# The opening norms of a two-layer kernel: fills moved to VectorE, a fixed order, and half of the norms moved into the loop

## The chip, the cores and the metric

The kernel runs on one core of one Trainium2 chip. Its engines are TensorE (PE in the profile; its weight loads are PEld), VectorE (DVE), ScalarE (ACT), GpSimd (POOL) and SyncE (SP, which only issues transfers). The engines run their own instruction streams in order and meet at semaphores. The metric is the device time of one execution in microseconds, lower is better; the time quoted is the median of several executions. A profile is one execution; its span runs from the first to the last instruction, and its time is a little longer than the span.

## The reference

The input `x` has 2 sequences of 1024 tokens with 128 features. Two pre-norm layers follow. Everything is float32. What this document turns on is the very first step and the layer that uses it:

```python
def _layernorm(x, axis=-1, eps=1e-05):
    m = jnp.mean(x, axis=axis, keepdims=True)
    v = jnp.var(x, axis=axis, keepdims=True)
    return (x - m) / jnp.sqrt(v + eps)
...
    x = x + _L0_attn_ref(_layernorm(x, axis=-1), ...)   # 16 heads of 64, causal
    x = x + _L0_ffn_ref(_layernorm(x, axis=-1), ...)    # a dense map and one of four low-rank maps for each token
    x = x + _L1_attn_ref(_layernorm(x, axis=-1), ...)   # 16 heads of 8, scores from squared distances
    x = x + _L1_ffn_ref(_layernorm(x, axis=-1), ...)    # a shared expert and 2 of 8 experts for each token
```

## The kernel before

Tokens are kept in tiles of 128 (16 tiles, 8 for each sequence) and in groups of four tiles, 512 tokens (four groups: 0 and 1 are the first sequence, 2 and 3 the second). The kernel has three parts.

**The opening** loads `x` and the weights, normalises `x`, turns weights around with TensorE, and projects the first unit. A unit is a pair of heads of one sequence, so each sequence has 8 units. The instructions of the opening are ordered by the framework's scheduler. `layernorm_T(b)` does the two groups of one sequence: for each of four token tiles `bn_stats` and `bn_aggr` (L134, L135), then the reciprocal square root (`rsqrt`: `bound` on DVE, L99; `guess` on ACT, a logarithm and an exponential, L102 and L103; `refine` on DVE, four small operations, L106 to L109), then for each tile the normalised tile `xn` (L141) and its transposition by TensorE (L145), and one copy of the four out of PSUM to `xnT` (L146). The opening calls it for the first sequence, projects the first unit from that (`project`, whose matmuls are all at the helper line L69, and whose results q, k and v leave PSUM at L432, L440 and L448), and calls it for the second sequence. `turn_nat` turns the 24 tiles of the q, k and v weights (L331) and copies them to `wqkvT` (L336, L338). `small_weights` turns and combines the other weights, with small results handed between PE, DVE, ACT and POOL (L153 to L409); its last result is `m2` (`m` in the profile, L409). `sides_of_rows` makes four small columns `side_of` for layer 1 from a tile `row`, which POOL zeroes, sets in parts and multiplies by the identity (L343 to L350), and DVE sums (L351). `fill(own[0], G)` zeroes 22 of every 32 columns of a big tile for layer 1 on POOL (L182, L183), and does not depend on anything.

PSUM is dealt out anew between the opening and the loop: the opening has four banks `tr` for transposed tiles and four `acc`; the loop has `sc`, `flip`, `z` and one bank `acc`. So the first matmul of the loop (`scp<-k,q`) waits until the last bank of the opening has been read out, which is the copy to `m2`.

**Layer 0's loop** is ordered by hand (`manual_schedule`), one step for each item; an item is a head pair's row block of 128 queries, `it["i"]` is the number of that block (0 to 7), and there are 128 items, those with `i` of 4 to 7 and of 0 to 3 taking turns. Each step runs the scores, the softmax (DVE L478, ACT L482, POOL L494), the transposition of the weights two steps later (`flip`, PE L512, copies L517), the sum with v (`zp`, L541), and in its last part one of three things in the bank `acc`: the end of a unit (`finish`), or the next piece of the next unit's projection (`later`), but none of these in a step whose `i` is 5. The second layer norm, the feed-forward part and the third norm of finished token tiles are dealt out over later steps as `events`, with the same `rsqrt_parts`.

**Layer 1** follows, attention and then the experts.

The queues matter for what follows. SP issues the loads of `x`, of the k weights, `proj`, the five plain weights, `wd` (four pieces), `wu` (eight pieces), and last `sim`, `bp` and `temp` (L309, L311, L313). POOL issues small loads too, as part of its own stream.

Of the kernel before, what the change touches and what calls it, by code (L numbers as in the profile page):

```python
# [14 lines left out]
P = 128  # L15
# [5 lines left out]
def two_layers(ctx: ExitStack, tc: tile.TileContext, a: dict, out: bass.AP):  # L21
# [40 lines left out]
    def tr():  # L62
        return bank("tr").rearrange("p o (j q) -> p (o j) q", q=P)
# [60 lines left out]
    def rsqrt(*of):  # L124
        for part in rsqrt_parts(*of)[:3]:
            part()


    def layernorm_T(b):
        for g in range(b * NG // B, (b + 1) * NG // B):  # L130
            mv = small.tile([P, 4, 2], FP, tag="mv", name="mv")
            for j in range(4):
                st = small.tile([P, V.BN_STATS_DIM], FP, tag="st", name="st")
                V.bn_stats(st, x[:, 4 * g + j, :])  # L134
                V.bn_aggr(mv[:, j, :], st)  # L135
            rstd = small.tile([P, 4], FP, tag="rstd", name="rstd")
            rsqrt(rstd, mv[:, :, 1], EPS, ALU.add)
            t = tr()
            for j in range(4):
                xn = work.tile([P, D], FP, tag="xn", name="xn")  # L140
                V.tensor_scalar(  # L141
                    xn, x[:, 4 * g + j, :], mv[:, j, 0:1], rstd[:, j : j + 1],
                    ALU.subtract, ALU.mult,
                )
                T.transpose(t[:, j, :], xn, ident)  # L145
            V.tensor_copy(xnT[:, bass.ts(g, 512)], t.rearrange("p j q -> p (j q)"))  # L146
# [92 lines left out]
    with ExitStack() as l0:  # L239
# [28 lines left out]
        def load_nat(eng, i, cs):  # L268
            w = a[f"L0_attn_W{'qkv'[i]}"].rearrange("h d e -> (h d) e").rearrange("(c p) e -> p c e", p=P)
            eng.dma_start(nat[i][:, cs, :], w[:, cs, :])  # L270

        for i in range(3):
            load_nat(nc.scalar, i, slice(0, 1))
        bnat = stage.tile([2 * NC, P], FP, name="bnat")
# [8 lines left out]
        load_nat(nc.scalar, 2, slice(1, NC))  # L283
        vnat = stage.tile([H, 2, DH], FP, name="vnat")
# [23 lines left out]
        simI = stage.tile([NP, 4 + NP], FP, name="simI")  # L308
        nc.sync.dma_start(simI[:, :4], a["L0_ffn_sim"])  # L309
        bp = stage.tile([NP, 1], FP, name="bp")  # L310
        nc.sync.dma_start(bp, a["L0_ffn_bp"].unsqueeze(1))  # L311
        temp = stage.tile([P, 1], FP, name="temp")
        nc.sync.dma_start(temp, a["L0_ffn_temp"].partition_broadcast(P))  # L313
# [25 lines left out]

        def sides_of_rows():  # L340

            row = stage.tile([P, 4, 4, 32], FP, name="row")
            G.memset(row, 0.0)  # L343
            for k, part, value in (
                (0, slice(0, DK), 1.0), (0, slice(DK + 1, DK + 2), 1.0), (1, slice(DK, DK + 1), 1.0),
                (2, slice(0, DK), 2.0), (2, slice(DK, DK + 1), 1.0), (3, slice(DK + 1, DK + 2), 1.0),
            ):
                G.memset(row[:, k, :, part], value)
            row = row.rearrange("p k h j -> p k (h j)")
            G.tensor_tensor(row, row, bcast(ident, 1, [P, 4, P]), ALU.mult)  # L350
            V.tensor_reduce(side_of, row, AX.X, ALU.add)  # L351
# [409 lines left out]
        turn_nat(*[(i, [0]) for i in range(3)])  # L761
# [3 lines left out]
        layernorm_T(0)  # L765
        for piece in project(units[0]):
            piece()
        layernorm_T(1)
# [6 lines left out]
        sides_of_rows()  # L775
# [11 lines left out]
        fill(own[0], G)  # L787
# [4 lines left out]
        while n < len(items) + LAG or longs or shorts or ends or later:  # L792
# [42 lines left out]
            elif later and not (it and it["i"] == 5):  # L835
                later.pop(0)()
            if old and old["i"] % 2:
                (longs if old["i"] >= 4 else shorts).extend(attend(old["group"]))
# [724 lines left out]
```

## Time and profile before

| | |
|---|---|
| time, median of 3 runs | 1074.09 us (1072.64 to 1076.69) |
| the profiled execution | time 1072.64 us, span 1070.9 us, mean granted TensorE clock 0.987 |
| busy in the span: PE / DVE / ACT / POOL | 1002.2 / 588.8 / 688.7 / 340.8 us |
| first matmul of the projection | starts at 17.67 us |
| first matmul of layer 0's loop | starts at 40.13 us |
| PE busy from 0 to 40 us, in stretches of 10 us | 1.68, 4.38, 9.73, 7.15 us |

The profile's page gives each engine's busy time and the span in 40 slices; further views give the chain of work that ended last (for each step the one before it that released it), a timeline in order of time, and groups of instructions by line and shape. In a group's row the numbers after the bar are the busy time in us and the mean of one instruction in ns. In a timeline row they are the start, the length in us, the engine, line and operation, output and inputs with partitions x elements, and how many instructions are merged into the row. Times of busy PE are modelled at their ends.

### The profile page before, as it was taken

Reading aid. Unit: us, or ns where it says so; the run is one execution under the profiler, and the core shown is the slowest. Engines: PE = TensorE matmul, PEld = TensorE weight load, DVE = VectorE, ACT = ScalarE, POOL = GpSimd, SP = SyncE. Lnnn points to the kernel's source line nnn. Section 1 sums busy time; section 2 is a strip of 40 time slices with the busy share of each in tenths; the row PEclk is TensorE's granted clock in tenths of the full one; section 3 lists DMA queues with packets and bytes.
Section 4 is the critical chain, followed back from the end, with each engine's and each line's share of the span. In section 5 each row is a group of like instructions: output and inputs, shape, how many; then the busy total and the mean of one; then the engine's idle time right before and its main releaser. Section 6 shows DMA issues by size and latency. Waiting matters only on the chain.

```text
span 1070.9 us, 26194 instructions
## 1 busy us (share of the span) xinstructions
PE 1002.2 (94%) x10662; PEld 603.2 (56%) x10662; DVE 588.8 (55%) x1758; ACT 688.7 (64%) x1312; POOL 340.8 (32%) x480
## 2 busy tenths in 40 slices
PE   4899999999999999999898989999999999899996
PEld 2466767667676676666666323323333332689885
DVE  7676677786877868686684333301434320455424
ACT  2376766666666666665465776888776778475651
POOL 4143343434444344444353020000000222005676
PEclk9799999999999999999999999999998999999999
DMA  5000000000000000000000500000000100011222
GB/s 131 1 2 2 2 2 2 2 2 2 2 3 2 2 2 2 2 2 1 2 2 15 164 1 2 1 1 1 21 2 6 28 18 19 1 40 46 70 72 75
DMA packets 27590, 20.13 MB, mean 19 GB/s; under 512 B 3715, under 2 KB 25070, under 8 KB 27470
## 3 DMA queue, kind: packets, MB, share of 16 engines
q1 hardware_dynamic: 22366, 12.17, 4.1%
q0 software_dynamic: 2816, 5.17, 1.7%
q8 instruction: 84, 1.38, 0.5%
q10 hardware_dynamic: 2288, 1.12, 0.4%
q14 instruction: 36, 0.29, 0.1%
HBM read 13.34 MB, written 5.11 MB: 17 GB/s over the span
## 4 chain that ended last, share of the span: by engine, by line
PE 75%; DVE 10%; ACT 7%; issue 3%; POOL 3%; DMA 2%; DVEq 0%; SPq 0%; POOLq 0%; ACTq 0%
PE accp L69 24%; PE bigp L69 14%; PE scp L69 11%; PE zp L69 10%; PE flipp L512 8%; PE trp L69 3%; ACT pT L517 2%; PE upp L69 2%; POOL back L1460 2%; ACT p L482 1%; DVE pT L517 1%; DMA xs<-rows,from 1%; PE trp L1217 1%; DVE p L478 1%; PE trp L208 1%
## 5 line engine op out<-in xcount | busy, mean ns | idle before, releaser
L1189 ACT ACTIVATE e<-bigp 128x1024 f32<-128x1024 f32 x256 | 247.7, 1021 | 79.6 <-PE bigp L69 66.5
L494 POOL TENSOR_SCALAR p<-p,rz 128x384 f32<-128x384 f32 (+7 forms) x256 | 188.2, 749 | 289.7 <-DVE rz L491 261.5
L482 ACT ACTIVATE p<-p,nmax 128x384 f32<-128x384 f32 (+7 forms) x256 | 196.3, 769 | 25.3 <-DVE nmax L478 24.5
L478 DVE CUSTOM_DVE_ANT_0 p<-scp,mask 128x384 f32<-128x384 f32 (+7 forms) x256 | 183.4, 753 | 28.0 <-PE scp L69 16.5
L517 ACT COPY pT<-flipp 128x128 f32<-128x128 f32 (+7 forms) x128 | 81.5, 636 | 146.9 <-PE flipp L512 140.0
L69 PE MATMUL scp<-k,q 64*128 64x512 f32 (+3 forms) x768 | 163.6, 505 | 0.5 <-DVE m L409 0.5
L69 PE MATMUL bigp<-rT,lT 32*128 32x512 f32 x1024 | 158.0, 643 | 0.0
L69 PEld LDWEIGHTS zp<-pT,v 128*64 128x64 f32 x2560 | 136.2, 137 | 26.9 <-issue 8.3
L69 PE MATMUL zp<-pT,v 128*64 128x128 f32 (+1 forms) x2560 | 146.5, 265 | 1.8 <-DVE zT L541 1.1
L512 PEld LDWEIGHTS flipp<-ident,p 64*128 64x128 f32 x2304 | 92.1, 139 | 97.9 <-issue 47.2
L69 PE MATMUL accp<-e,own 128*32 128x512 f32 x1024 | 140.5, 611 | 0.0
L517 DVE COPY pT<-flipp 128x128 f32<-128x128 f32 (+7 forms) x128 | 96.0, 750 | 58.7 <-PE flipp L512 58.5
L512 PE MATMUL flipp<-ident,p 64*128 64x64 f32 x2304 | 111.1, 229 | 17.8 <-DVE rz L491 14.5
L1053 POOL DMA_INDIRECT xs<-rows,from x46 | 45.6, 991 | 239.2 <-DVE top L1073 156.9
L69 PEld LDWEIGHTS bigp<-rT,lT 32*128 32x128 f32 x1024 | 50.6, 183 | 108.2 <-issue 71.5
L69 PEld LDWEIGHTS scp<-k,q 64*128 64x128 f32 x768 | 69.9, 190 | 38.0 <-issue 30.8
L69 PE MATMUL accp<-xnT,wqkvT 128*64 128x512 f32 x256 | 71.7, 627 | 1.7 <-ACT o L619 0.8
L1316 ACT ACTIVATE hs<-upp,w 128x128 f32<-128x128 f32 x176 | 50.3, 369 | 33.3 <-PE upp L69 16.3
L69 PEld LDWEIGHTS accp<-e,own 128*32 128x32 f32 x1024 | 20.9, 108 | 65.4 <-issue 64.6
L432 ACT ACTIVATE q<-accp,bqk 128x512 f32<-128x512 f32 x32 | 37.2, 1163 | 29.7 <-PE accp L69 29.1
L1206 DVE COPY cs<-accp 128x512 f32<-128x512 f32 x16 | 11.0, 690 | 73.0 <-PE accp L69 73.0
L541 DVE TENSOR_TENSOR zT<-zp,bz 128x256 f32<-128x256 f32 x64 | 38.7, 605 | 20.9 <-PE zp L69 20.6
(330 smaller groups left out, 1148.2 us busy)
## 6 DMA issues: line engine op xcount, KB each, us to landing
given<-y SPq DMA_DIRECT2D x10, 256.0 KB, 2.3
wx<-in_L_ffn_We_dram SPq DMA_DIRECT2D x1, 2048.0 KB
wx<-in_L_ffn_We_dram SPq DMA_DIRECT2D x8, 256.0 KB, 4.0
x<-in_L_attn_x_dram SPq DMA_DIRECT2D x4, 256.0 KB, 4.0
rows<-xn SPq DMA_DIRECT2D x4, 256.0 KB, 2.3
out_dram<-x SPq DMA_DIRECT2D x3, 256.0 KB, 2.3
xs<-rows,from POOLq DMA_INDIRECT x46, 2.5
proj<-in_L_attn_proj_dram SPq DMA_DIRECT2D x1, 512.0 KB
```

The costliest lines, as they stand in the source:

```text
L69: T.matmul(o, lhsT=lhsT, rhs=rhs, start=start, stop=stop)
L432: S.activation(q[:, 4 * j : 4 * j + 4].rearrange("p i r u -> p i u r"), t.rearrange("p (i u r) -> p i u r", r=2, u=DH), AF.Identity, bias= ...
L478: V.tensor_tensor_reduce(out=p[:, :n], in0=it["sc"][hh], in1=mask[:, SEQ - n :], scale=1.0, scalar=-NEG, op0=ALU.add, op1=ALU.min, accum_o ...
L482: S.activation(p[:, :n], p[:, :n], AF.Exp, bias=nmax, scale=-1.0, accum_out=it["sum"][:, hh : hh + 1],)
L494: G.tensor_scalar(p[:, :n], p[:, :n], r[:, hh : hh + 1], SC, ALU.mult, ALU.mult)
L512: T.transpose(it["t", hh][:, r, j, :], it["p"][hh][rs, bass.ts(j, P)], ident[rs, rs])
L517: copy(it["group"]["pT", hh][:, : i + 1, i % 2].rearrange("p j r u -> p r j u"), it["t", hh])
L541: V.tensor_tensor(zT[:, :, :, 16 * g : 16 * g + 16].rearrange("p m h q -> p h q m"), z.rearrange("p (h q m) -> p h q m", h=2, m=M2), bz[:, ...
L1053: G.indirect_dma_start(out=r["xs"][q][:, j, :], out_offset=None, in_=rows[b][:, :], in_offset=bass.IndirectOffsetOnAxis(ap=r["from"][:, i ...
L1189: S.activation(e[:, 2 * pr : 2 * pr + 2, :], sc[pr], AF.Exp, scale=1.0 / math.sqrt(DK))
L1316: S.activation(h[:, f, :], t[:, f, :], AF.Silu, bias=w[:, I + NF * D + f : I + NF * D + f + 1])
L1460: G.indirect_dma_start(out=returned[b, j][:, k, :], out_offset=None, in_=given[b][:, :], in_offset=bass.IndirectOffsetOnAxis(ap=routed[b][ ...
```

## The change

It has four parts.

1. `fill(own[0], V)`: the big tile's fill is issued at the start of the opening, on VectorE. The tile `row` is zeroed and set in parts on VectorE as well; its product with the identity stays on GpSimd, now near the head of its stream. The sum `side_of` stays on VectorE.
2. The loads of `sim`, `bp` and `temp` go from the end of SP's queue to GpSimd's, ahead of its other small loads.
3. In the opening only groups 0 and 1 are normalised. `norm_T(g)` returns three parts (statistics and guess; refine, normalise and transpose; copy). They are issued with VectorE and ScalarE in a fixed order: both groups' statistics first, then group 0, with the first three weight tiles between, then group 1.
4. Groups 2 and 3 are normalised in layer 0's loop by `norm_later`: one piece in each step after the eighth whose `i` is below 4 (a tile's statistics, or the guess, or one tile normalised into a free part of `xn2T`), and the four transpositions with ScalarE's copy in the bank `acc`, in a step in which neither `finish` nor `later` uses it.

The core of the diff, in the changed kernel's order (the old `layernorm_T`, `sides_of_rows` and the three SP loads are taken out):

```diff
+    def norm_T(g):
+        mv = small.tile([P, 4, 2], FP, tag="mv", name="mv")
+        rstd = small.tile([P, 4], FP, tag="rstd", name="rstd")
+        bound, guess, refine = rsqrt_parts(rstd, mv[:, :, 1], EPS, ALU.add)[:3]
+        t = []
+
+        def stats():
             for j in range(4):
                 st = small.tile([P, V.BN_STATS_DIM], FP, tag="st", name="st")
                 V.bn_stats(st, x[:, 4 * g + j, :])
                 V.bn_aggr(mv[:, j, :], st)
+            bound()
+            guess()
+
+        def normal():
+            refine()
+            t.append(tr())
             for j in range(4):
                 xn = work.tile([P, D], FP, tag="xn", name="xn")
                 V.tensor_scalar(
                     xn, x[:, 4 * g + j, :], mv[:, j, 0:1], rstd[:, j : j + 1],
                     ALU.subtract, ALU.mult,
                 )
+                T.transpose(t[0][:, j, :], xn, ident)
+
+        def keep():
+            V.tensor_copy(xnT[:, bass.ts(g, 512)], t[0].rearrange("p j q -> p (j q)"))
...
+    def norm_later(g, room):
...
+        def guess():
+            stats(3)
+            w["rstd"] = small.tile([P, 4], FP, tag="rstd", name="rstd")
+            w["parts"] = rsqrt_parts(w["rstd"], w["mv"][:, :, 1], EPS, ALU.add)
+            w["parts"][0]()
+            w["parts"][1]()
+
+        def normal(j):
+            if not j:
+                w["parts"][2]()
+            V.tensor_scalar(
+                room[:, bass.ts(j, P)], x[:, 4 * g + j, :], w["mv"][:, j, 0:1], w["rstd"][:, j : j + 1],
+                ALU.subtract, ALU.mult,
+            )
+
+        def turn():
+            t = spare[0]()
+            for j in range(4):
+                T.transpose(t[:, j, :], room[:, bass.ts(j, P)], ident)
+            spare[1](xnT[:, bass.ts(g, 512)], t.rearrange("p j q -> p (j q)"))
+
+        each = lambda f, js: [lambda j=j: f(j) for j in js]
+        return each(stats, range(3)) + [guess] + each(normal, range(4)) + [turn]
...
         for i in range(3):
             load_nat(nc.scalar, i, slice(0, 1))
+        fill(own[0], V)
+
+        row = stage.tile([P, 4, 4, 32], FP, name="row")
+        V.memset(row, 0.0)
...
+            V.memset(row[:, k, :, part], value)
+        row = row.rearrange("p k h j -> p k (h j)")
+        G.tensor_tensor(row, row, bcast(ident, 1, [P, 4, P]), ALU.mult)
...
+        nc.gpsimd.dma_start(simI[:, :4], a["L0_ffn_sim"])
...
+        nc.gpsimd.dma_start(bp, a["L0_ffn_bp"].unsqueeze(1))
...
+        nc.gpsimd.dma_start(temp, a["L0_ffn_temp"].partition_broadcast(P))
...
-        turn_nat(*[(i, [0]) for i in range(3)])
+
+        with tc.manual_schedule(engines={mybir.EngineType.DVE, mybir.EngineType.Activation}):
+            one, two = norm_T(0), norm_T(1)
+            one[0]()
+            two[0]()
+            one[1]()
+            turn_nat(*[(i, [0]) for i in range(3)])
+            one[2]()
+            two[1]()
+            two[2]()
         transposed(bqk, bnat)

         V.tensor_scalar(bqk[:, :NC], bqk[:, :NC], -SC, None, ALU.mult)
-        layernorm_T(0)
         for piece in project(units[0]):
             piece()
-        layernorm_T(1)
...
-        sides_of_rows()
+        V.tensor_reduce(side_of, row, AX.X, ALU.add)
...
-        fill(own[0], G)
+        norms = []
+        for g in range(NG // B, NG):
+            norms += [(False, f) for f in norm_later(g, xn2T[:, bass.ts(g, 512)])]
+            norms[-1] = (True, norms[-1][1])
...
             elif later and not (it and it["i"] == 5):
                 later.pop(0)()
+            elif norms and norms[0][0]:
+                norms.pop(0)[1]()
+            if norms and not norms[0][0] and it and it["i"] < 4 and n > NB:
+                norms.pop(0)[1]()
```

The order of the instructions on each engine, as built, adds three things that the diff alone doesn't tell. On DVE the operations on `simI` and `temp` (the tiles of the loads that change queue) stand inside the norms: `simsq`, which reads `sim`, stands behind the first of group 1's refine operations, and the one on `temp` ahead of group 1's last `xn`. On PE the first head of the first projection stands ahead of group 1's first three transpositions, and the second head behind them; then two q weight tiles, group 1's last transposition, five more q tiles and three k tiles, then the other six of the projection's matmuls. In the loop, TensorE gets four transpositions of `xn2T` into `accp` at two places, and nothing else is moved there.

More of the change, by code (lines that the diff above doesn't have):

```diff
@@ L126, in rsqrt @@
             part()
-    def layernorm_T(b):
-        for g in range(b * NG // B, (b + 1) * NG // B):
-            mv = small.tile([P, 4, 2], FP, tag="mv", name="mv")
+    def norm_T(g):
[4 more added lines that the diff above has]
+        def stats():
             for j in range(4):
@@ L135, in layernorm_T @@
                 V.bn_aggr(mv[:, j, :], st)
-            rstd = small.tile([P, 4], FP, tag="rstd", name="rstd")
-            rsqrt(rstd, mv[:, :, 1], EPS, ALU.add)
-            t = tr()
+            bound()
[3 more added lines that the diff above has]
+            t.append(tr())
             for j in range(4):
@@ L144, in layernorm_T, with stats @@
                 )
-                T.transpose(t[:, j, :], xn, ident)
-            V.tensor_copy(xnT[:, bass.ts(g, 512)], t.rearrange("p j q -> p (j q)"))
+                T.transpose(t[0][:, j, :], xn, ident)
+        def keep():
+            V.tensor_copy(xnT[:, bass.ts(g, 512)], t[0].rearrange("p j q -> p (j q)"))
+        return stats, normal, keep
+    def norm_later(g, room):
+        w = {}
+        def stats(j):
+            if not j:
+                w["mv"] = small.tile([P, 4, 2], FP, tag="mv", name="mv")
+            st = small.tile([P, V.BN_STATS_DIM], FP, tag="st", name="st")
+            V.bn_stats(st, x[:, 4 * g + j, :])
+            V.bn_aggr(w["mv"][:, j, :], st)
+        def guess():
[5 more added lines that the diff above has]
+        def normal(j):
+            if not j:
+                w["parts"][2]()
[10 more added lines that the diff above has]
+        return each(stats, range(3)) + [guess] + each(normal, range(4)) + [turn]
     def transposed(dst, src):
@@ L273, in two_layers @@
             load_nat(nc.scalar, i, slice(0, 1))
+        fill(own[0], V)
+        row = stage.tile([P, 4, 4, 32], FP, name="row")
+        V.memset(row, 0.0)
+        for k, part, value in (
+            (0, slice(0, DK), 1.0), (0, slice(DK + 1, DK + 2), 1.0), (1, slice(DK, DK + 1), 1.0),
+            (2, slice(0, DK), 2.0), (2, slice(DK, DK + 1), 1.0), (3, slice(DK + 1, DK + 2), 1.0),
+        ):
+            V.memset(row[:, k, :, part], value)
+        row = row.rearrange("p k h j -> p k (h j)")
+        G.tensor_tensor(row, row, bcast(ident, 1, [P, 4, P]), ALU.mult)
         bnat = stage.tile([2 * NC, P], FP, name="bnat")
@@ L283, in two_layers @@
         load_nat(nc.scalar, 2, slice(1, NC))
+        simI = stage.tile([NP, 4 + NP], FP, name="simI")
+        nc.gpsimd.dma_start(simI[:, :4], a["L0_ffn_sim"])
+        bp = stage.tile([NP, 1], FP, name="bp")
+        nc.gpsimd.dma_start(bp, a["L0_ffn_bp"].unsqueeze(1))
+        temp = stage.tile([P, 1], FP, name="temp")
+        nc.gpsimd.dma_start(temp, a["L0_ffn_temp"].partition_broadcast(P))
         vnat = stage.tile([H, 2, DH], FP, name="vnat")
@@ L307, in two_layers @@
                 )
[L308 to L313, printed above, removed]
         nc.gpsimd.dma_start(wr1, a["L1_ffn_Wr1"])
@@ L338, in turn_nat @@
                 V.tensor_copy(wqkvT[:, :, cs[0] * P : (cs[0] + 1) * P], t[:, :at, :])
[L340 to L351, printed above, removed]
         def small_weights():
```

## The prediction

> **What bounds the kernel now.** I read the page first, then the chain of waits of the opening and of the loop, then the timelines of DVE and POOL for the first 45 us. The page says that TensorE is the bound of the whole:
>
> ```profile
> PE 1002.2 (94%) x10662; PEld 603.2 (56%) x10662; DVE 588.8 (55%) x1758; ACT 688.7 (64%) x1312; POOL 340.8 (32%) x480
> ```
>
> That mean hides the opening. There the chain is DVE's until 17.6 us (start, length, what):
>
> ```profile
> 8.94 0.17 DVE rsq L99
> 9.10 0.21 DVE rsq L106 x3
> 9.31 0.22 DVE rsq L107 x3
> 9.53 3.92 DVE rsq L108 x3
> 13.45 0.03 DVE rstd L109
> 13.47 1.31 DVE rstd L109 x2
> 17.67 1.97 PE accp L69 x2
> 22.65 4.47 PE accp L69 x44
> 30.18 2.60 DVE wqkvT L336 x5
> 39.70 0.30 DVE m L409
> ```
>
> Operations on 4 columns take 3.92 and 1.31 us here. In POOL's timeline the same stretches are its fills and its product:
>
> ```profile
> 9.98 0.54 POOL L343 MEMSET row<- 128x512 f32 x1
> 10.44 2.46 POOL L182 MEMSET own<- 128x2816 f32 x1
> 12.83 0.35 POOL L348 MEMSET row<- 128x32 f32 x6
> 13.49 1.27 POOL L350 TENSOR_TENSOR row<-row,ident 128x512 f32<-128x512 f32 x1
> ```
>
> L108 ends at 13.45 as the fills end, L109 at 14.78 as the product ends (14.76): DVE is held by POOL for about 5 us, with everything behind it. In the loop the chain of 75 to 250 us has DVE for under 3%:
>
> ```profile
> by line: PE scp L69 26.3%; PE zp L69 26.0%; PE accp L69 19.8%; PE flipp L512 18.6%; ACT pT L517 4.0%; issue 1.5%; DVE pT L517 1.0%; DVE rz L491 0.6%; ACT p L482 0.6%; DVE rsq L107 0.4%; DVE rsq L106 0.3%; DVE p L478 0.2%; DVE st L571 0.1%;
> ```
>
> **The fills on DVE.** DVE's own fills give the price:
>
> ```profile
> L369 DVE MEMSET ones<- 32x128 f32 x1 | 0.2, 165 | 0.9 <-PEq L1549 0.9
> L385 DVE MEMSET brow<- 128x51 f32 x1 | 0.1, 101 | 0.0
> ```
>
> 77 elements more cost 64 ns, so 0.83 ns each and 0.06 us fixed (1.04 ns if the fixed part is 0.04 us). 2816 elements are 2.4 to 3.0 us, I take 2.9; `row` 0.55, the 128-element piece 0.1, six small pieces 0.4. DVE starts at 0.89, so ends near 4.9, where before it began the statistics at 4.00 when `x` had landed. Cost 0.9 us.
>
> **The opening in the fixed order.** A dependent `bn_stats` and `bn_aggr` take 0.42 us a tile (the loop's pair at 633.01 is followed by the next at 633.43), against 0.26 us interleaved in the opening now. Eight tiles with two bounds: 4.9 + 3.6 = 8.5. ACT's guess of group 0 (two of 0.2 us) hides under group 1's statistics. `refine` is four dependent steps of 0.2 (18.30, 18.48, 18.68 show the spacing): 9.35. Three `xn` at 0.26 (rows 0.34 long, overlapping): 10.1; `side_of` 0.6 (the row is 0.67, POOL's product done at about 6.3): 10.7; the fourth `xn`: 11.0; the copy of the first weight tiles 0.5 (row 0.54): 11.5; `xnT` 0.7 (row 0.69): 12.2. The first head's matmul starts at 12.25 instead of 17.67, 5.4 us earlier.
>
> Then PE's order decides. The first head took 1.97 us alone at 17.67, so 14.2; three transpositions and the bias 1.1 (L145 x3 took 0.99 at 15.10): 15.3; the second head 1.97 if TensorE is as slow as at 20.19, 1.1 if it is as fast as after 22.6 (two heads together took 1.08 at 47.31). Two q tiles and group 1's last transposition 0.3 to 0.6, the copy 0.7, three k tiles behind it (their bank is freed by that copy) 0.4: the six other matmuls start between 18.15 and 19.2, where now it is 22.58. Gain 3.9, the middle; ends 3.4 and 4.4.
>
> The rest of the projection is unchanged and ends at 27.05 now. From there to the end of the `wqkvT` copies DVE has 5.65 us (to 32.7): two `xnT`, three `xn`, six copies. Afterwards the q tiles are copied earlier and the second sequence isn't there; four copies stay (0.6, 0.5, 0.6, 0.5) and 0.2 for the first tile: 2.4. Gain 3.25 more, together 7.15. From 32.7 to 40.13 the chain of small weights is the same hand-to-hand work, 7.4 us, and the loop starts near 33.0.
>
> **The loads that change queue.** POOL issues them behind the product and `mask`, at about 7.0, 7.6 and 8.1. POOL's loads issued at 7.18 to 8.20 landed after 5.9 to 6.0 us, in the crowded first 15 us; `sim` and `temp` on SP took 1.6 and 2.6 late in the opening. So they land at 13.0 and 14.1. Behind `simsq` on DVE wait the other three refine steps of group 1, and PE for their tiles; but PE has the first head until 14.2, and the tiles come at 13.6 to 14.4. Cost nothing; without that cover each us of delay costs one. If they land as late as POOL's slowest (6.5 us and issued a us later), 1.5 us are lost.
>
> **The loop.** Eight transpositions go from the opening to a loop that TensorE bounds. Seven tiles took 0.93 us at 27.43: 0.13 each, 1.05 us. Statistics 8 x 0.42 and `xn` 8 x 0.34 are 6.1 us of DVE over some 170 us in which DVE is busy 75%; I cost them at nothing, hidden under PE's matmuls; statistics are never held (259 to 293 ns, 32 of L571). The small operations can be: L106 and L107 together are 0.7% of 175 us on the chain, 1.2 us for the three or four norms in it, 0.35 a set. Two sets: 0.7. ACT's two copies (0.57, the row of v) fall in steps with an empty `acc`: nothing, at worst 0.6 each. Sum 1.75; bounds 0.8 (half the transpositions hidden, half the holds) and 6.
>
> **Sum.** -7.15 + 1.75 = -5.4: a span of 1065.5 and a time of 1067.2 for an execution like the profiled one (1072.64, the fastest shown, 1.45 under the median). Against the median 1074.09 I predict 1068.6, 0.5% less. A measurement of this kernel can tell 0.5% (5.4 us) from no change; the forecast lies on that edge.
>
> [...] The clock row comes first:
>
> ```profile
> 32.00:33.00 1.00, 0.49 (x3) 0.31 (x2) 1.00 (x5) 0.00 (x0) 0.00 (x0) 0.81 0.05 16
> 33.00:34.00 1.00, 1.00 (x4) 0.54 (x3) 0.79 (x6) 0.00 (x0) 0.00 (x0) 0.50 0.00 0
> 46.00:47.00 1.00, 1.00 (x10) 0.52 (x8) 0.36 (x2) 0.90 (x1) 0.07 (x1) 0.86 0.00 0
> ```
>
> (the seventh number is the granted clock) shows half speed from 32.6 to about 46.3, so 6.1 us of the loop run slow. [...]
>
> For the loads the row is POOL's 5.9 us against SP's 1.6. [...]
>
> **The rivals.**
> *Late loads* (0.12): `sim` lands past 14.2 and DVE stands at `simsq`. For: nothing else in the fixed order can pass it, and POOL's last load (6.5 us) was slower than all but three of SP's (`raw_w` 7.8, `raw_wp` 7.4, `raw_wv` 6.6). Against: 13.0 by the nearest rows. Priced at 2 to 3 us: about 1071.
>
> *The loop pays for all* (0.25): the transpositions, ACT's copies and some held `xn` reach PE, 4 us instead of 1.75: 1071. For: `xn` copies SBUF to SBUF like the operations held at 9.53. Against: DVE waits 24.0 us for `flip` in that window, so there is slack.
>
> *Held norms in the loop turn the change over* (0.09): L99, L106 and L107 have single instances of 1020, 942 and 1025 ns, 0.85 above the least. Eighteen operations (eight `xn`, two bounds, eight of refine) held that long and all passed on to PE are 15.3 us: -7.15 + 1.05 + 15.3 = +9.2, 1083. Slower than before as soon as more than 6.1 us of the holds pass through. Against: the medians of L106 and L107 on `rstd` are 155 and 161 ns, so most are not held.
>
> *The fill still holds someone* (0.05): if DVE's fill keeps POOL out as POOL's kept DVE out, POOL's product starts later, near 7.5, and blocks the first refine: 1 to 2 us, 1070. Either way the 5 us hold is gone.
>
> **How the numbers follow.** The forecast as it stands has 0.49. Its own spread, 1 us from the second head, 1 from the phase, 1 from the loop, puts it half on either side of the 0.5% edge, towards the faster side where ACT and DVE are wholly hidden (1066) and the opening takes its upper end (1065). Faster by over 0.5%: 0.47; within: 0.44 (the rest of the forecast and the first, second and fourth rivals); slower by over 0.5%: 0.09, the third. Range 1064 to 1075: the best ends of opening and loop, up to a loop that takes back the whole gain.
>
> **What would show it.** In the changed profile: no operation of L106 to L109 over 0.3 us before 15 us; DVE's fills from 0.9 to 4.9; the first projection matmul at 12.2, the six others at 18 to 19, the loop at 33. POOL's product at 5 to 6.3. `simsq` without a wait for its load. In the loop, PE's chain longer by 1 to 2 us between 75 and 250, `xn` at 0.34 or held. It would be wrong if the loop starts later than 35, or if the loop, from its start to the end, is longer by over 3 us.

## The result, and the profile after

The kernel after takes 1067.91 us (median of 4 runs, 1067.13 to 1069.35), the kernel before in the same comparison 1075.39 (1072.64 to 1076.75): a ratio of 0.994, 95% interval 0.9922 to 0.9958. The profiled executions have spans of 1066.4 and 1070.9 us, so the two traces that are compared below are 4.5 us apart, where the medians are 7.5 us apart: the trace before is the fastest of its four executions.

TensorE's busy time in the summary of the kernel after is what it was (1002.2 us before):

```profile
PE 1001.5 (94%) x10662; PEld 604.1 (57%) x10662; DVE 588.9 (55%) x1765; ACT 689.2 (65%) x1314; POOL 338.5 (32%) x474
```

The chain of waits of its opening (start, length, what):

```profile
1.47 2.40 DVE own L228
...
8.61 0.18 DVE rsq L108
8.81 0.17 DVE rstd L109
...
12.29 1.97 PE accp L69 x2
...
15.30 1.90 PE accp L69 x2
...
18.60 4.47 PE accp L69 x44
23.37 2.23 DVE wqkvT L393 x4
...
32.18 0.30 DVE m L453
32.62 0.80 PE scp L69 x4
```

The operations of L108 and L109 that took 3.92 and 1.31 us now take 0.18 and 0.17. The first projection matmul starts at 12.29 (17.67 before), the other six heads' at 18.53 by the timeline (22.58), the loop's first scores at 32.62 (40.13). That is 7.5 us by the loop's start. GpSimd's product, beside which L109 stood before, now runs while VectorE has only statistics to do, whose `bn_stats` take 0.26 us each beside it (timeline of GpSimd, the bracket is the idle time ahead of it and who ended it):

```profile
4.87 1.26 POOL L330 TENSOR_TENSOR row<-row,ident 128x512 f32<-128x512 f32 x1 [1.83 <-DVE row L328]
```

The loop gives some of it back. The chain of the loop from 75 to 250 us:

```profile
by line: PE zp L69 25.6%; PE scp L69 24.4%; PE accp L69 19.4%; PE flipp L556 17.3%; ACT pT L561 4.0%; issue 2.0%; DVE pT L561 2.0%; PE accp L188 0.7%; ACT p L526 0.6%; DVE p L522 0.6%; DVE rz L535 0.6%; DVE rsq L107 0.5%; DVE rsq L99 0.5%; 
```

New in it is `accp L188`, the eight transpositions: 0.7% of 175 us, 1.2 us. VectorE's operations of the norms are on this chain for about 4 us, summed over their lines, where they were for 2 before; L99 and the normalising (L180) are most of the difference.

How far the kernel after is ahead at the same piece of work (the last addition to `x` of a unit, and layer 1's start and end) shows where the rest went:

| point | before, us | after, us | ahead by |
|---|---|---|---|
| loop's first scores | 40.13 | 32.62 | 7.51 |
| unit 5 finished | 262.73 | 256.61 | 6.12 |
| unit 11 finished | 465.94 | 459.67 | 6.26 |
| unit 15 finished | 586.03 | 580.31 | 5.72 |
| end of the span | 1070.93 | 1066.44 | 4.49 |

No instruction that the change moved into the loop runs behind unit 11. What takes 1.8 us there are two stretches of 3.4 us at half the granted clock that the profile before does not have: at the same instructions the lead falls from 6.24 to 5.72 us across the first and from 5.73 to 4.54 across the second, and from there to the end it stays between 4.5 and 5.1. The windows of the kernel after show them (stretch, its length, the busy time of PE, PEld, DVE, ACT and POOL, the granted clock, the DMA share, GB/s):

```profile
467.80:471.20 3.40, 1.40 (x18) 0.74 (x13) 3.19 (x11) 0.55 (x2) 1.83 (x3) 1.00 0.00 0
471.20:474.60 3.40, 3.10 (x34) 2.68 (x36) 1.70 (x6) 1.91 (x5) 1.35 (x2) 0.51 0.00 0
631.60:635.10 3.50, 1.60 (x18) 0.34 (x10) 0.65 (x4) 3.47 (x6) 0.87 (x2) 1.00 0.00 0
635.10:638.50 3.40, 3.32 (x20) 0.93 (x20) 0.42 (x1) 0.05 (x1) 2.05 (x10) 0.50 0.00 0
```

A window in which TensorE was busy for 1.40 of 3.40 us is followed by one at half clock. In the kernel before the same dip falls between two windows, none of them so empty, and nothing follows:

```profile
472.90:476.30 3.40, 2.54 (x38) 1.70 (x34) 3.16 (x13) 1.69 (x5) 2.89 (x4) 1.00 0.00 0
476.30:479.70 3.40, 1.80 (x34) 1.55 (x36) 2.83 (x7) 1.21 (x3) 1.43 (x3) 1.00 0.00 0
```

### The profile page after: what moved, and what is told of

It reads as the page before. It is cut to its first block, busy times and chain, and to the rows that moved or that the text cites. A ratio compares the mean times of both kernels' runs of the same rounds, so it can differ in the third digit from the quotient of the medians.

```text
span 1066.4 us, 26197 instructions
## 1 busy us (share of the span) xinstructions
PE 1001.5 (94%) x10662; PEld 604.1 (57%) x10662; DVE 588.9 (55%) x1765; ACT 689.2 (65%) x1314; POOL 338.5 (32%) x474
## 4 chain that ended last, share of the span: by engine, by line
PE 75%; DVE 10%; ACT 6%; issue 3%; POOL 3%; DMA 2%; DVEq 0%; POOLq 0%; ACTq 0%
PE accp L69 24%; PE bigp L69 14%; PE scp L69 10%; PE zp L69 10%; PE flipp L556 8%; PE trp L69 3%; PE upp L69 2%; ACT pT L561 2%; DVE pT L561 2%; POOL back L1520 2%; DMA xs<-rows,from 2%; ACT p L526 1%; PE trp L1277 1%; DVE p L522 1%; PE trp L254 1%
## 5 line engine op out<-in xcount | busy, mean ns | idle before, releaser
L556 PE MATMUL flipp<-ident,p 64*128 64x64 f32 x2304 | 111.4, 229 | 17.4 <-DVE rz L535 13.8
```

Of the source, the lines that this page charges most:

```text
L556: T.transpose(it["t", hh][:, r, j, :], it["p"][hh][rs, bass.ts(j, P)], ident[rs, rs])
```

## The experiments

Parts of the change are numbered as in the section on the change: 1 the fills, 2 the loads, 3 the fixed order, 4 the norms in the loop. In the comparisons of the first four kernels and the next four the kernel before took 1073.8 and 1074.4 us. In that of the last four, on the same chip as the second, the kernels that were measured twice, before included (1086.45), took 10 to 12 us more, so only its ratios and its own pairs are used. A head here is one head's q or k for one group of tokens; the first two heads are the pair's q for group 0. The bracket behind a time is the ratio to before with its interval.

### One part at a time

**Part 1 alone** (the kernel before with both fills on VectorE):

```diff
+        fill(own[0], V)
+        row = stage.tile([P, 4, 4, 32], FP, name="row")
+        V.memset(row, 0.0)
...
-        fill(own[0], G)
```

> The kernel before with part 1 alone: both fills on VectorE at the start, GpSimd's product near the head of its stream; loads, norms and order as before. Theory (a held VectorE sets the opening, and its end moves everything behind it): no operation of L106 to L109 over 0.3 us before 15 us, first projection matmul at 12.5 to 13.5 instead of 17.67, layer 0's loop at 35 to 36 instead of 40.13, the time 4 to 5 us under before (ratio 0.9955 to 0.9965). Rival 1 (the hold only changes its place): another VectorE operation of 1 us or more on the chain before 20 us, loop start at 38 or later, gain under 2 us. Rival 2 (VectorE's 3.2 us of fills cost what the hold cost): xn starts no earlier than 13.

1070.1 us (0.9968, 0.9956 to 0.9981). First matmul 11.56, six others 17.05, loop 35.73: 4.4 us earlier, and no operation on four columns is held (0.16 us at most). The first matmul came earlier than the 12.5 to 13.5 that were expected, and the time fell by 3.7 us, not by 4 to 5. The hold was real and this part takes it away by itself.

**Part 1 undone** (after, with both fills on GpSimd again, where they were):

```diff
-        fill(own[0], V)
-        V.memset(row, 0.0)
...
+        G.memset(row, 0.0)
...
+        fill(own[0], G)
```

> The changed kernel with part 1 undone: both fills and the product on GpSimd where they were, the rest as changed. Theory (the hold is 5 us, but what it costs depends on which operation it meets): GpSimd fills from about 9.5 to 14.8 us; group 0's norm is done before, group 1's refine is held instead, while TensorE has the first two heads; loop start at 33 to 35 (32.62 in the changed kernel), the time 0.5 to 2 us over the changed kernel. Rival (the hold is what the change removed, and its return costs all of it): loop start at 37 to 38, 5 us over the changed kernel.

1069.92 us (0.9963, 0.9949 to 0.9977), loop at 34.78. The hold is back, later and on group 1 (timelines of VectorE and of GpSimd):

```profile
12.25 0.16 DVE L107 TENSOR_TENSOR rsq<-rsq,rstd 128x4 f32<-128x4 f32 x1
12.44 3.72 DVE L108 TENSOR_SCALAR rsq<-rsq 128x4 f32<-128x4 f32 x1
...
16.40 1.43 DVE L148 TENSOR_SCALAR xn<-x,mv,rstd 128x128 f32<-128x128 f32 x2
```

```profile
12.70 0.54 POOL L816 MEMSET row<- 128x512 f32 x1
13.16 2.46 POOL L228 MEMSET own<- 128x2816 f32 x1
```

L108 ends at 16.16 as GpSimd's fills end (16.14). It costs 2.2 us of the loop's start, not 4.4, since the first head is already on TensorE when it strikes. What a hold costs depends on which operation it meets.

**Part 4 undone** (after, with groups 2 and 3 normalised in the opening):

```diff
+        for g in range(NG // B, NG):
+            for part in norm_T(g):
+                part()
...
-            norms += [(False, f) for f in norm_later(g, xn2T[:, bass.ts(g, 512)])]
```

> The changed kernel with part 4 undone: groups 2 and 3 normalised in the opening behind the first projection, nothing of it in the loop. Theory (VectorE's copies stand between the projection and the small weights): loop start 3 to 3.5 us later than the changed kernel, 35.6 to 36.1; from the loop's start to the end of layer 0 1.3 to 1.8 us less than the changed kernel, so the time 1.5 to 2 us over it, 1069.5. Rival (the opening hides them): loop start within 1 us of 32.6 and the time 1 us under the changed kernel.

1072.35 us (0.9977, 0.9965 to 0.9989), loop at 37.41: the deferral saves 4.8 us of the opening, where 3 to 3.5 were expected, and the time is 4.4 us over after's, not 1.5 to 2. From the loop's start to unit 5 this kernel takes 222.0 us, after 224.0. Of the 4.8 us, 3.4 come behind the projection, where VectorE's work for groups 2 and 3 stands, as the theory had it. The other 1.4 are TensorE's pace (timelines of VectorE and of TensorE):

```profile
14.70 0.15 DVE L418 TENSOR_SCALAR temp<-temp 128x1 f32<-128x1 f32 x1 [0.98 <-DMA temp<-in_L_ffn_temp_dram]
```

```profile
18.26 4.44 PE L69 MATMUL accp<-xnT,wqkvT 128*64 128x512 f32 x12 [0.29 <-DVE xnT L155]
```

The six others start no later than in after, but take 4.44 us instead of 2.80. VectorE has statistics of groups 2 and 3 between those of 0 and 1 here and stands for `temp`, one of part 2's loads, before it normalises group 1, so that TensorE idles. The kernel is also slower than part 1 alone (35.73), although it has more of the change: a first sign that parts 2 and 3 are not free, without telling which of them costs.

**Part 2 undone** (after, with the three small loads at the end of SP's queue):

```diff
-        nc.gpsimd.dma_start(simI[:, :4], a["L0_ffn_sim"])
...
+        nc.sync.dma_start(simI[:, :4], a["L0_ffn_sim"])
```

> The changed kernel with part 2 undone: the loads of sim, bp and temp at the end of SyncE's queue. Theory (the 0.6 us wait for sim is hidden under the first head's matmul): six other projection matmuls at 18.3 to 18.8, loop start at 32.4 to 32.9, no difference in time (ratio to the changed kernel 0.999 to 1.001). Rival 1 (a load from GpSimd's queue is late and costs): loop start 0.5 to 1.5 us earlier. Rival 2 (the loads are needed earlier than SyncE brings them, at 20 us): simsq waits to 20 or later and stands before group 1's refine, loop start 5 us or more later.

1068.74 us (0.9948, 0.9932 to 0.9965), loop at 32.56 against 32.62. Issued by SP at 19.5 the load of `sim` takes 1.6 us, issued by GpSimd at 6.69 it is there at 12.9. The cover is seen directly: group 1 is normalised from 12.94 instead of 13.57, and TensorE turns it at 14.2 in both, when the first head is done. But the equal start of the loop is two differences that cancel (timelines of TensorE and of VectorE):

```profile
17.80 2.79 PE L69 MATMUL accp<-xnT,wqkvT 128*64 128x512 f32 x12
```

```profile
23.07 0.15 DVE L418 TENSOR_SCALAR temp<-temp 128x1 f32<-128x1 f32 x1 [1.09 <-DMA temp<-in_L_ffn_temp_dram]
```

The six others start 0.73 us earlier than in after, also earlier than the 18.3 to 18.8 expected, because the second head takes 1.28 us instead of 1.97; in an order that is the same up to there, that is the execution's pace and not the loads. VectorE then stands 1.09 us for `temp`, and the copies behind it (L393) end only 0.24 us ahead of after's (the rest goes in the small weights, with half clock from 25.93 instead of 27.51). So loads at the end of SP's queue do cost some 0.5 us here, by this reading of one trace; neither rival had that.

### The order, the loop's price, the place of the fill, and a full order

**Part 3 undone**: VectorE and ScalarE are ordered by the scheduler, the rest is after.

```diff
-        with tc.manual_schedule(engines={mybir.EngineType.DVE, mybir.EngineType.Activation}):
+        if True:
```

> The kernel after, but the opening's norms of groups 0 and 1 are ordered by the scheduler on VectorE and ScalarE; fills on VectorE, loads on GpSimd and the norms of groups 2 and 3 in the loop stay. Theory (the opening's gain is the hold that goes and the VectorE work that leaves; the order itself is worth little): the interleaved statistics save some 0.8 us, the six other matmuls start at 17.5 to 19, the loop starts between 31.5 and 34 (after: 32.6), and the time is 1067 to 1069. Rival (the fixed order is what makes the parts add up): the six others start past 21, the loop at 35 or later, time 1070 or more. In both the loop costs the same 1.8 us from its start to the finish of unit 5 as in after (224.0 against 222.6 before).

1063.77 us (0.9904, 0.9882 to 0.9927): better than after. The two intervals still overlap by a little; the pair measured side by side below settles it. First matmul 11.91, six others 16.46, loop 30.54. All are earlier than the theory's (six others 17.5 to 19, loop 31.5 to 34, time 1067 to 1069): what it took for worth little, the order, costs 2 us. Why is seen in TensorE's timeline of this kernel,

```profile
11.30 0.69 PE L388 MATMUL trp<-ident,nat_q 128*128 128x128 f32 x2
11.91 1.97 PE L69 MATMUL accp<-xnT,wqkvT 128*64 128x512 f32 x2
13.81 0.69 PE L152 MATMUL trp<-ident,xn 128*128 128x128 f32 x2
14.43 1.07 PE L69 MATMUL accp<-xnT,wqkvT 128*64 128x512 f32 x2
```

and that of the kernel after:

```profile
12.29 1.97 PE L69 MATMUL accp<-xnT,wqkvT 128*64 128x512 f32 x2 [1.03 <-DVE xnT L155]
14.19 0.90 PE L152 MATMUL trp<-ident,xn 128*128 128x128 f32 x3
15.02 0.28 PE L198 MATMUL trp<-ident,bnat 16*128 16x16 f32 x1
15.23 1.97 PE L69 MATMUL accp<-xnT,wqkvT 128*64 128x512 f32 x2
```

With the order free, TensorE turns q tiles, the bias and a tile of group 1 ahead of the first head, where after it stands idle for 1.03 us; and the second head takes 1.07 us instead of 1.97.

TensorE has reached full pace by 14.43 in the one, by 17.2 in the other (the granted clock reads 1.00 in both all that time; the pace is read from the length of a head). In the profile of after the stretches at half clock begin at 27.50, 471.23, 635.07, 812.56 and 966.16 us and are 10.24, 3.41, 3.41, 6.83 and 3.41 us long; the lengths, and the distances from one start to the next, are whole multiples of 3.41 us (130, 48, 52 and 45 of 3.413). A window here is one such length of 3.41 us, counted back from these starts into the opening. In these three kernels full pace comes at the end of the first window of 3.41 us through which TensorE has worked without a gap: 11.05 to 14.46 without the order, 13.86 to 17.27 in after, 19.02 to 22.43 before (PE busy 3.41, 3.41 and 3.43 us in them; 2.32, 2.38 and 2.88 in the windows ahead). A window without any gap is not needed: with group 1 ahead of the copies, below, it comes at 17.28, after a window with 2.98 us busy.

By these lines 0.4 of the 2.07 us at the six others are the earlier first head, 0.9 the second head's pace, and 0.8 the small operations: the bias and one transposition that after has between the heads (1.04 us from one head to the next, 0.62 here), and two q tiles and one transposition that it has behind them (1.40, 1.02 here). The 0.9 belongs to these two executions: the second head took 1.28 and 1.72 us in two others with after's order up to there.

**Only the transpositions in the loop.** The statistics, guess and normalising of groups 2 and 3 are empty pieces:

```diff
-                T.transpose(t[:, j, :], room[:, bass.ts(j, P)], ident)
+                T.transpose(t[:, j, :], x[:, 4 * g + j, :], ident)
...
-        return each(stats, range(3)) + [guess] + each(normal, range(4)) + [turn]
+        return [lambda: None] * 8 + [turn]
```

> The kernel after, but in the loop the pieces with the statistics, the guess and the normalising of groups 2 and 3 are empty and the transpositions read the tiles of x themselves: the second sequence is not normalised. Theory (of the loop's price, 1.05 us is TensorE's eight transpositions and 0.7 us the held operations on VectorE): from the loop's start to the finish of unit 5 it takes 223.0 to 223.5, between before (222.6) with 222.0 in the runs without the deferral, and after (224.0, 223.7 in two other runs with it); so about 0.6 us less than after, and the time 1067.2. Rival one (the held operations are nearly all of it): 222.2 and a time of 1066.4. Rival two (the transpositions with ScalarE's copy are all of it): 223.7 to 224.0, no change against after.

1067.78 us (0.9942, 0.9919 to 0.9965). From the loop's start to unit 5 it takes 223.67 us. That alone would speak for rival two, but this execution has 5.6 us of half clock inside the loop, the others 3.6 to 6.1. A line through the 13 other profiles has a slope of 0.30 us for each us of half clock, and a step of 1.73 us between the kernels with the deferral and those without; none is off it by more than 0.13. By that line the transpositions, with ScalarE's copies, are 1.25 of the 1.73, VectorE's part 0.48. The theory had 1.05 and 0.7.

**The fill on GpSimd, but early:**

```diff
-        fill(own[0], V)
+        fill(own[0], G)
```

> The kernel after, but the big tile is filled by GpSimd at the head of its stream, where after has it on VectorE; the tile row stays on VectorE. Theory (what costs is an operation that is held, not the engine of the fill; the fill on GpSimd from about 1 us is done at 4 to 5, when VectorE has only statistics to do, which were never held): no operation on four columns is held over 0.3 us before 15 us, the statistics start at 4.0 instead of 4.6, the loop starts at 32.0 to 33.0, the time is that of after within 1 us. Rival (the product, which follows the fill on GpSimd's queue, comes 1.5 us later and meets group 0's operations on four columns): one of them is held for 0.5 to 1.3 us, the first projection matmul starts at 12.8 to 13.6, the loop at 33.2 to 34.

1067.0 us (0.9938, 0.9913 to 0.9962), loop at 31.24. GpSimd fills from 2.99 to 5.42 and multiplies from 6.48; VectorE's statistics, which run beside both, take 0.26 to 0.33 us, one bound 0.40, and the other operations on four columns 0.15 to 0.17. The theory holds for the hold: a fill on GpSimd held nobody here, where it met only statistics. Its numbers for the start did not: the statistics start at 4.29, when `x` has landed, and the loop 0.8 us earlier than expected and 1.4 earlier than after's. That comes with the scheduler's order of the rest, which changed with it, and with the clock. One more weight copy is done before the projection ends (0.6 us), the small weights run longer ahead of the half clock (from 28.48, 27.51 in after; 0.7 us), and on TensorE the first two heads stand in a row (timeline of TensorE):

```profile
12.49 1.98 PE L69 MATMUL accp<-xnT,wqkvT 128*64 128x512 f32 x4 [1.25 <-DVE xnT L155]
```

The two take 1.98 us together, where in after each of them, with transpositions between, takes 1.97. So the order that parts the two heads paid for one of them twice. Here the six others still start only 0.3 us earlier than in after (18.20), behind transpositions at slow pace.

**A full order**, also of TensorE, meant to beat after; the core of it:

```diff
+            refine0(), normal0(), turn0()
+            st1(3), ag1(2), ag1(3)
...
+            q0()
+            refine1(), normal1(), turn1()
+            keep1()
+            k0(), v0()
+            turn_nat((1, range(1, 5)))
+            q1()
...
```

> A kernel that goes further than after: the whole opening's order on TensorE, VectorE and ScalarE is written out. The statistics of two tiles are interleaved, group 0 is normalised ahead of group 1's last statistics, group 0's q weights are projected before group 1 is turned, the k and q weight tiles are turned between the pieces of the projection, the merged weights come early, and row is set on GpSimd; the deferral to the loop stays. Theory (the opening is bound by the chain of VectorE's operations and TensorE's transpositions handing over to each other, not by the loads): the first projection matmul starts at 11 to 11.5, the loop at 27.5 to 29.5, so 3 to 5 us earlier than after, and the time is 1063 to 1065. Rival (the loads of the weights, the last of which land past 14 to 16 us, set the order): TensorE stands for raw weights, the loop starts at 31 or later and the time is within 1.5 us of after.

1067.29 us (0.9943, 0.9921 to 0.9965). The first matmul starts at 11.62 and the heads of k and v at 14.59, but the loop at 30.26, outside the forecast of 27.5 to 29.5, and the time is not the 1063 to 1065 that were expected: the small weights, from VectorE's copy at 24.73 on, take 5.5 us hand to hand and stand behind projection pieces and weight tiles on TensorE. Beside the kernel without the order (loop at 30.54) only 0.3 us is won there, and the time is 3.5 us longer; its runs have 30 to 34 us of half clock each, those of the other 21 to 26.

### What the order costs, and the pace of TensorE

**Group 1 ahead of the copies:**

```diff
             one[1]()
+            two[1]()
             turn_nat(*[(i, [0]) for i in range(3)])
             one[2]()
-            two[1]()
             two[2]()
```

> The kernel after, but in the opening's fixed order group 1 is refined and normalised right behind group 0, ahead of the copies of the first weight tiles and of group 0's transposed tiles. Theory (the order written in after is dear because group 1's norm stands behind group 0's copies and, through simsq, behind the load of sim; its last transposition is then behind a slow head on TensorE): group 1 is normalised by 11.7 instead of 15.05, the first projection matmul starts later (13 to 14.4, behind the load of sim at 12.9), but all heads then run in a row and the loop starts at 30.5 to 32.0, 0.6 to 2 us before after's 32.6. Rival (an early first head is what counts, and the wait for sim now stands ahead of it): the loop starts at 32.6 or later.

1080.73 us (0.9947, 0.9927 to 0.9967), loop at 31.71. Group 1 is normalised by 12.8 and all heads run in a row from 15.42, later than expected because the first copies stand behind the load of `sim` (13.28) and four q tiles ahead of the head; still the loop starts 0.6 us before that of after in the same comparison (32.32). Theory, at its weak end; the time is not told apart from after's.

**TensorE kept busy from the start** (the kernel without the order, and seven matmuls that nobody reads):

```diff
+        warm = acc()
+        for _ in range(7):
+            mm(warm, ident, bcast(ident, 1, [P, 4, P]))
```

> The kernel without the opening's fixed order (e5), with seven matmuls of 128x512 on the identity added at the head of TensorE's stream, whose result nobody reads. Theory (TensorE works at half speed until the end of the first window of 3.41 us that it has worked through, which after's first heads paid with 1.97 us instead of 1.08): the seven take 5 to 7 us from about 2, inside them one passes to the faster pace, transpositions of 128x128 then follow at 0.13 instead of 0.21 us and the first head takes 1.1 us; the six other matmuls start at 14.5 to 15.7 (e5: 16.5), the loop at 29 to 30. Rival (the next windows, with short transpositions and waits for VectorE, are too idle to keep the pace): the first head takes 1.97 us again and the loop starts at 30.5 or later. Half the granted clock shows again before the loop starts in both.

1081.66 us (0.9962, 0.9951 to 0.9974), loop at 33.98. The rival's numbers came out, but not for its reason: the scheduler's order of VectorE changed with it and put the operations on `sim` and `temp` behind the first three `xn`, ahead of all others (timeline of VectorE):

```profile
12.93 0.15 DVE L411 TENSOR_TENSOR simsq<-simI 32x4 f32<-32x4 f32 x1 [3.18 <-DMA simI<-in_L_ffn_sim_dram]
14.14 0.15 DVE L418 TENSOR_SCALAR temp<-temp 128x1 f32<-128x1 f32 x1 [1.06 <-DMA temp<-in_L_ffn_temp_dram]
```

So it shows something else, the price of the loads without their cover: 4.2 us of VectorE, 4.3 of TensorE, which stood until 14.61. The seven took 7.83 us, not 5 to 7. TensorE's pace did rise (their matmuls are 0.85 us apart at first and 0.43 from 5.3 on; transpositions 0.11 us apart from 9.6, 0.21 in the others at that time), then the window from 11.9 to 15.3, in which TensorE was busy for 0.7 us, was followed by one at half clock (15.3 to 18.7), in which the first head took 1.97 us again. What an early pace is worth by itself stays open.

**After, and the kernel without the order, again:**

> The kernel after, unchanged, on the chip of this comparison: the yardstick for the two kernels without the fixed order. Theory (the windows of 3.41 us run free, so each execution meets the dips of TensorE's work at another place): the loop starts within 1 us of 32.6, the half clock at the loop's start ends with the first window that lies wholly in the loop, and the windows at half clock in mid-run are others than those at 471 and 635 of the first profile. Rival (these windows belong to the kernel's own schedule): they are again at 471 and 635. Time 1067 to 1069 in both.

> The kernel without the opening's fixed order (e5), unchanged, a second time beside after. Theory (the order itself costs about 2 us): the loop starts at 30 to 31.5, the time is 3 to 4.5 us under after's in the same comparison. Rival (e5's lead was the place of its free-running windows: a fast first head at 14.4 and no window at half clock in mid-run): the loop starts at 31.5 or later and the time is less than 2 us under after's.

After: 1080.11 us (0.9945, 0.9926 to 0.9964; not the 1067 to 1069 expected, as said above of this comparison), loop at 32.32, half clock in mid-run at 634.4 to 641.2 and none at 471. The half clock at the loop's start begins at 26.80, in the first profile at 27.50, so the windows lie 0.70 us earlier; the one ahead of 470.5 has TensorE busy for 47%, the one ahead of 471.2 in the first profile for 40%. The dips are the kernel's, where the windows fall on them is the execution's. The execution with group 1 ahead of the copies, whose windows happen to lie as in the first profile of after (half clock from 27.5 in both), has the same two, at 471.3 and 635.1.

Without the order: 1073.8 us (0.9889, 0.987 to 0.9909), loop at 29.71 (0.3 us earlier than the 30 to 31.5 expected), second head 1.07 us at 14.25. The lead is 2.6 us at the loop's start and 2.3 at unit 15, which is the order, with the second head's pace in it. The medians are 6.3 us apart, more than the 3 to 4.5 of the theory.

In the two traces the lead grows behind unit 15 by 1.6 us at 640, where after has the longer stretch at half clock, by 1.6 at about 820, where only after has one, and by 2.1 at the stop that the last section describes; 0.6 are lost between 645 and 800. The timed runs have 30 to 37 us of half clock against 41 to 54. At some 0.3 us for each us (the slope within either kernel's own runs lies between 0.24 and 0.40) that is some 3 of the 4 us that the order doesn't explain. Why nine runs of nine without the order have less of it, though the windows lay elsewhere in the second profile of either kernel, was not settled.

## Why the prediction was right

The forecast was 1068.6, measured 1067.91. The mechanism, a held VectorE ahead of the projection, was right; that the sum came out so close is in part luck, as the steps show:

1. *The hold.* Right: L106 to L109 take 0.15 to 0.17 us, and part 1 alone and undone shows the hold go and return. VectorE's own fill holds nobody: beside it GpSimd's fill of `mask` takes 0.94 us (L296, from 2.10), as it does in the kernel before, and the product starts at 4.87, ahead of the first refine, so that rival is out.
2. *The fills, 0.9 us.* 0.6: VectorE starts them at 1.47, not 0.89, but fills 2816 elements in 2.40 us (0.85 ns each, the lower end of the bounds), and the statistics begin at 4.63 instead of 4.00 (4.29 in the run with the fill on GpSimd, where they wait for `x`).
3. *First matmul 12.25, six others 18.15 to 19.2, loop near 33.0.* 12.29, 18.53 and 32.62. The gain of 7.15 was 7.5.
4. *The loads, hidden.* Right for this kernel: `sim` came at 12.9 (13.0 was said), and `simsq` waited 0.60 us under the first head; "`simsq` without a wait for its load" was not met. Part 2 undone starts the loop at the same time, but by two differences that cancel, so what part 2 is worth is not measured to better than half a microsecond. The rival of late loads was wrong by its cover, not by its price: without that cover they cost 4.2 us of VectorE in the kernel with seven more matmuls, and 0.98 us with part 4 undone. In the kernel after `sim` was there 6.2 us after GpSimd issued it at 6.69, with part 2 undone 1.6 us after SP issued it at 19.5. No run issues it on both queues at the same time, so what the 6.2 us are owed to was not shown.
5. *The loop, 1.75 us.* 1.73 over 13 profiles, split 1.25 (ScalarE's copies in it) to 0.48 instead of 1.05 to 0.7. Statistics in the loop take 0.27 us, not held. `xn` is held somewhat (0.44 on average, 0.83 at most) and the hold mostly lies under TensorE's work. With that the loop that pays for all, and held norms that turn the change over, are out.
6. *The clock, left out of the sum.* Here the sum was short. No run shows the 1 us "from the phase" in the forecast's spread. In its place the 14 profiles show half clock until 3.6 to 6.1 us after the loop's start, which at 0.30 us for each us (the slope over 13 profiles) is some 0.8 us between the ends (an estimate from these numbers), and the two windows at half clock in mid-run took 1.8 us of the profiled execution. So the gain between the two traces was 4.5 us, not 5.4, and the ratio of the timed runs says 4.5 to 8.4, which holds 5.4: a hit whose last term is chance from one execution to the next.
7. *The chances.* They do not add up as written: half of 0.49 on either side of the 0.5% edge makes 0.25 for faster and 0.66 for within, not 0.47 and 0.44. The measured gain is 0.6%, with an interval of 0.4% to 0.8%, so it lies on that edge too.

What no step of it said: the order itself. The sum priced its steps well as they stand, and asked of none whether another order would be shorter: 2.1 to 2.6 us at the loop's start were left lying, as TensorE's idle time, two heads that run one after the other, and slow pace. A row that told part of it was there: statistics 0.26 us apart in the opening before, 0.42 as taken for the fixed order (0.40 measured); the first `xn` starts 0.8 us earlier without it (8.22 against 9.01).

## What to carry to other kernels

Where a few small operations take microseconds, look at what the other vector engine runs at that time, and move that work to when only untouched operations run; here L108 went from 3.92 us to 0.18, and the moved work held nobody on either engine. Before an order is written by hand, try the same parts without it: here three of the four parts are worth 1%, and the fourth takes about 0.2% back by the loop's start, and 0.4% to 0.6% in the medians, where the rest goes mostly with time at half clock. A run that changes nothing may hold two differences that cancel, so follow it through the stages. A difference of under half a per cent needs several executions and their time at half clock beside it.

## What the runs showed of the hardware

In all 14 profiles the half clock at the loop's start ends with the first window of 3.41 us that lies wholly in the loop, 3.6 to 6.1 us after its start. Where the windows lie differs from execution to execution: by 0.70 us between the two profiles of after, by 0.41 between the two without the order. Between 400 and 800 us the windows followed by half clock had TensorE busy for 33% to 54%; some of 47% to 56% were followed by none. In the opening, full pace came behind windows with TensorE busy for 87% (group 1 ahead of the copies) and 93% (with the seven matmuls), and not behind one of 84% (before). The runs also show half clock at about 810 (all profiles but one) and 965 (all), behind windows in which TensorE was busy for 96% to 100%, so there it came without an idle window ahead of it; why was not shown.

A microsecond at half clock cost 0.30 us at the loop's start. In the two windows of 3.41 us in after it cost 0.15 (at 471, 0.52 us in all) and 0.35 (at 635, 1.19 us). Two heads in a row took 1.98 us at slow pace and 1.08 at full pace, one head alone 1.97 and 1.07.

In the last comparison the times were 10 to 12 us longer, on a chip where they had not been, and in the traces it came at the end: the kernel after reached unit 15 at 579.3 us (580.3 in the first comparison), then ScalarE stood for 15.15 us from 1036.9 ahead of its L1472, and for 13.7 to 13.8 us near there in the other three. The profiles of the other comparisons have 6.18 us at that line. The cause is not known.
